# A graph-convolution kernel: groups gathered ahead from group 44 on, and tiles paired in one group of four

## The chip, the cores and the metric

The kernel runs on one core of a Trainium2 chip. Its engines work side by side, each through its own list of instructions in order: PE (TensorE, matmuls; its weight loads are listed apart as PEld), DVE (VectorE), ACT (ScalarE), POOL (GpSimd) and SP (SyncE, which issues loads and stores). The metric is the device time of one execution in microseconds; lower is better. The times before are the median of three runs.

## The reference

A layer of a graph network with 12500 nodes of 128 features and 400000 edges, sorted by `dst`:

```
h    = relu(layernorm(x))
W    = smu(edge_attr @ W_f1.T + b_f1) @ W_f2.T + b_f2      # smu: gelu-like, 20 -> 128 -> 128
W    = W * edge_weight[:, None]
msg  = (h @ W_in2f.T)[dst] * W                             # one message of 128 floats per edge
agg  = segment_sum(msg, src, 12500)                        # src is in no order
out  = x + smu(agg @ W_o1.T + b_o1) @ W_o2.T + b_o2
```

(In the code `src` and `dst` enter `_L0_gnn_ref` as `idx_i` and `idx_j`.) The gather goes by the sorted index, the sum by the random one.

## The kernel before

**Tiles, groups, epochs.** 128 edges make a tile, four tiles a group, two groups a super. There are 3125 tiles in 782 groups. The 98 blocks of 128 nodes are called bins. The sum over a random index is made in two passes: each message is first scattered to DRAM, into a buffer that is sorted by bin (`buf`), at a place counted out on the chip; later the buffer is read back bin by bin (`rw`), and a matmul with a one-hot matrix (`se`) adds up the rows of each node. `PARTS` cuts the edges into ten epochs, and while an epoch is scattered, the epoch before it is read back and summed (`add`, L1017). The supers of the last two epochs are spread among the others as "kept" groups: their messages wait in DRAM, and are scattered in a tail behind the last group.

**One group** takes these steps, each of which is a function of the group:

- `hide`, `bend`: the hidden layer (PE, L779, into the PSUM tile `pu`) and its gelu (ACT `ge`, L787);
- `pick_part`: the one-hot matrix `oh` for the gather (ACT, L578 and L579);
- `gather`, `take`: the rows of h by matmuls with `oh` (PE `ph`, L815) and their copy with the edge's weight (ACT `hg`, L834);
- `weigh`, `mix`: the filter (PE `pw`, L859 and L860) and the product (DVE `ms`, L889);
- `bins`, `count`, `read`, `number`: the place of each message within its bin (DVE `so`, L614; PE `pc`; DVE `sl`, L671; DVE `ix`);
- `send`, `scatter`: one indirect DMA a tile from POOL (L959) that writes 128 message rows to their places.

Messages have six buffers (`ms`), places (`ix`) eight.

**Pairs.** In one of `EVERY` groups, the messages of tiles 2 and 3 are moved into the rows of tiles 0 and 1 whose message goes into the same bin, so that one DMA writes two neighbouring rows. `spread_keys` (PE, L705) and `match` (DVE, L714, L719) find the partners, `rank_left` (PE, L726) and `place_left` (DVE, L733, L734) number those that have none, `permute` (PE, L746) moves the rows by matmuls into the PSUM tile `pt`, and `take_pairs` copies them out: `ms` (ACT, L759) for the second row of each pair, and `lt` (ACT, L760) for the left-over messages, with two small DVE instructions (`lat`, L756 and L757) for their bin and row. The left-overs are scattered with a later group, its `host`, and counted with it (L622). A paired group thus takes two double scatters, and its host one more.

**Order.** The kernel writes the order of every engine by hand: the loop over `p` calls the steps of different groups in a fixed order, and each engine takes its part of it in that order. Up to `p = AHEAD_FROM` the loop gathers and copies group p + 1, for which the product `mix(p + 1)` follows in the same turn. From there on it gathers p + 2, and hides and bends p + 3. Behind group 112, where `AHEAD_FROM` stands, the hidden layer takes turns in the PSUM banks `pu` and `pg1`, and the sums have `pg0` alone; before it, `pu` is alone and `pg0` and `pg1` take turns. `parts` puts off the start of a new bank of sums while `pu` has two banks. In the first epoch (up to group 112) there are no sums yet; there the loop does the preparation in small `step`s: layernorm and the rows of h, the reading of indices, the splitting of the edge features.

Of the kernel before, what the change touches and what calls it, by code (L numbers as in the profile page):

```python
# [15 lines left out]
ALU = mybir.AluOpType  # L16
# [14 lines left out]
GRP = 4  # L31
WIN = 42
PARTS = (56, 56, 56, 56, 46, 36, 36, 26, 16, 7)
EVERY = 5
WIDER = 0.17
SENT_LAST = 2
BUFS = 3
# [1 line left out]
ROW = P + 1  # L39
# [3 lines left out]
NOBIN = 200.0  # L43
NOBIN_ROW = float(1 << 17)
# [3 lines left out]
def gnn_kernel(  # L48
# [19 lines left out]
    nc = tc.nc  # L68
# [14 lines left out]
    PER = SUP // GRP  # L83
    NG = (NT + GRP - 1) // GRP
    eps_of, left = [], NS
# [9 lines left out]
    for a, n in eps_of:  # L95
        paired = n if len(CAP) < len(eps_of) - SENT_LAST else 0
# [100 lines left out]
    drow = const.tile([P, EPOCHS], F32, name="drow")  # L197
# [124 lines left out]
    with tc.tile_pool(name="ld", bufs=4) as ld, \  # L322
# [24 lines left out]
        pu_names = ["pu"]  # L347
# [151 lines left out]
        def at(p):  # L499
            return seq[p] if p < len(seq) else NG  # L500
# [10 lines left out]
        for p, g in enumerate(seq):  # L511
            if g // PER >= EARLY:
                continue
            since_pair += 1
            if wanting and p >= wanting[0][0] + 4:
                host[g] = wanting.pop(0)[1]
                assert epoch[g // PER] == epoch[host[g] // PER]
            elif since_pair >= EVERY and g > BY and g + 10 < ends_of[epoch[g // PER]]:
                paired[g] = len(paired)
                wanting.append((p, g))  # L520
                since_pair = 0
# [47 lines left out]
        def pick_part(g):  # L569

            if g >= NG:
                return
            s, i = divmod(g, PER)
            if i == 0:
                onehot[s] = edge.tile([P, SUP * P], BF, name="oh", bufs=3)
            o, n = i * GRP * P, groups[g][1] * P
            oh = onehot[s][:, o:o + n]
            nc.scalar.activation(oh, loaded[s][1][:, o:o + n], AF.Abs, bias=pneg if s < FEW // SUP else nrow)  # L578
            nc.scalar.activation(oh, oh, AF.Relu, scale=-1.0, bias=onesb[:, 0:1])  # L579
# [4 lines left out]
        def s_of(g):  # L584
            return g // PER
# [143 lines left out]
        def place_left(g):  # L729
# [5 lines left out]
                                    irow_ps.unsqueeze(1).to_broadcast([P, 2, P]),  # L735
                                    at_.unsqueeze(2).to_broadcast([P, 2, P]), op=ALU.is_equal)

        def permute(g):

            pp, cd = matched.pop(g)[1], apart_of.pop(g)  # L740
            po = ps1.tile([P, GRP * P], F32, name="pt")
            for j in range(3):
                w = ROW + 2 if j == 2 else ROW
                for i in range(2):
                    o = (4 + i if j == 2 else 2 * i + j) * P
                    nc.tensor.matmul(po[:, j * (ROW + 2):j * (ROW + 2) + w], pp[:, o:o + P], cd[:, i, :w],  # L746
                                     start=(i == 0), stop=(i == 1))
            matched[g] = po

        def take_pairs(g):  # L750

            po, ms, k = matched.pop(g), mixed[g], epoch[s_of(g)]
            lt = cnt.tile([P, ROW], F32, name="lt", bufs=2)
            at_ = cnt.tile([P, 2], F32, name="lat")
            o = 2 * (ROW + 2)
            nc.vector.tensor_scalar(at_[:, 0:1], po[:, o + ROW:o + ROW + 1], NOBIN, None, op0=ALU.add)  # L756
            nc.vector.tensor_scalar(at_[:, 1:2], po[:, o + ROW + 1:o + ROW + 2], NOBIN_ROW, drow[:, k:k + 1],  # L757
                                    op0=ALU.add, op1=ALU.min)
            nc.scalar.activation(ms[:, 1::2, :], po[:, :o].rearrange("p (j r) -> p j r", j=2)[:, :, 0:ROW], AF.Copy)  # L759
            nc.scalar.activation(lt, po[:, o:o + ROW], AF.Copy)  # L760
            left_of[g] = (lt, at_[:, 0:1], at_[:, 1:2])
# [28 lines left out]
        def smooth(g):  # L790
            if g >= NG:
                return
            if new(g):
                units_of.pop(g)
                return
            n = groups[g][1] * P
            sm = edge.tile([P, GRP * P], F32, name="sm", bufs=3)
            nc.vector.scalar_tensor_tensor(sm[:, :n], units_of.pop(g)[:, :n], LIN, hidden[g][:, :n],
                                           op0=ALU.mult, op1=ALU.add)
            hidden[g] = sm  # L800
# [25 lines left out]
        def take(g):  # L826
            if g >= NG:
                return
            n = groups[g][1] * P
            hg = edge.tile([P, GRP * P], F32, name="hg")  # L830
            if by_edge(g):
                t = groups[g][0]
                for j in range(groups[g][1]):
                    nc.scalar.activation(hg[:, j * P:(j + 1) * P], rows_of[g][:, j * P:(j + 1) * P], AF.Copy,  # L834
                                         scale=w_sb[:, t + j:t + j + 1])
                rows_of[g] = hg
                return
            nc.scalar.activation(hg[:, :n], rows_of[g][:, :n], AF.Copy)
            rows_of[g] = hg
# [77 lines left out]
        def send(g):  # L917

            if by_edge(g):
                scatter(g, mixed.pop(g))  # L920
                return
            t, n = groups[g]
            ms = msg.tile([P, GRP, ROW], F32, name="ms")
            places_in(g, ms)
            pt = mixed.pop(g)
            for j in range(n):
                nc.scalar.activation(ms[:, j, 0:P], pt[:, j], AF.Copy, scale=w_sb[:, t + j:t + j + 1])
            if s_of(g) >= EARLY:
                nc.scalar.dma_start(kept_rows[:, t - kept_tile:t - kept_tile + n, :], ms[:, :n, :])
                return  # L930
            scatter(g, ms)
# [543 lines left out]
            todo.setdefault(10 + i, []).append(f)  # L1475

        k = 0
        SOON, SLACK, AHEAD_FROM = 10, 40, eps_of[1][0] * PER
        for p in range(len(seq)):
            g = seq[p]  # L1480
            s = g // PER
            if p == (FEW // SUP - 3) * PER:
                assert not opening
            if p % PER == 0:
                load(sup_at(p // PER + 3))
            if s < EARLY:
                k = chores(g)
            else:
                lo = hi = done
            if SOON < p < SLACK:  # L1490
                turn(at(p))
                send(at(p))
            if p >= SLACK:
                if by_edge(g) and g not in paired:
                    send(g)
                if p > SLACK and not by_edge(at(p - 1)):
                    turn(at(p - 1))
                    send(at(p - 1))
            for f in todo.pop(p, []):
                f()  # L1500
            if p > AHEAD_FROM:
                smooth(at(p + 2))
            step()
            number(at(p + 1))
            weigh(at(p + 1))
            if at(p + 1) in paired:
                spread_keys(at(p + 1))
            if p <= AHEAD_FROM:
                gather(at(p + 1))
                take(at(p + 1))  # L1510
            parts(lo + (hi - lo) // 2)
            mix(at(p + 1))
            if g in paired:
                permute(g)
                take_pairs(g)
                send(g)
            if at(p + 1) in paired:
                match(at(p + 1))
            if p >= AHEAD_FROM:
                gather(at(p + 2))  # L1520
                take(at(p + 2))
            if p == 0:
                turn(at(1))
                send(at(1))
            if p >= SOON:
                step()
            if p <= AHEAD_FROM:
                hide(at(p + 2))
                bend(at(p + 2))
            else:  # L1530
                hide(at(p + 3))
                bend(at(p + 3))
            if p < SOON:
                step()
            count(at(p + 2))
            if p <= AHEAD_FROM:
                smooth(at(p + 2))
            if 0 < p < SOON:
                turn(at(p + 1))
                send(at(p + 1))  # L1540
                if p == 1:
                    pick_part(at(3))
            if p == AHEAD_FROM:
                assert taken_steps == COUNT
                pu_names[:] = ["pg1", "pu"]
                hide(at(p + 3))
                bend(at(p + 3))
            pick_part(at(p + 3 - (p == 0)))
            bins(at(p + 3))
            if at(p + 1) in paired:  # L1550
                rank_left(at(p + 1))
            read(at(p + 2))
            if at(p + 1) in paired:
                place_left(at(p + 1))
            parts(hi)
            step()
            assert k == 0 or taken_steps == COUNT
# [291 lines left out]
```

## Time and profile before

| | |
|---|---|
| runs | 4022.95, 4025.37, 4024.81 us; median 4024.81 |
| profiled execution | 4014.04 us, span 4012.3 us |
| busy share of the span | PE 83%, DVE 81%, POOL 74%, ACT 71% |
| mean granted clock of TensorE | 0.946 |
| scatters on POOL (L959) | 2694 + 181 of kept rows + 125 of left-overs |

The profile has a page for the whole execution and views that answer questions: groups of instructions by line, waits (who stood idle, for whom, how long in total, how many times, longest), busy time by windows, a timeline. "L959" is line 959 of the kernel before; `out<-in` names the tiles; x is a count. A scatter's time as counted on POOL does not hold the transfer itself.

### The profile page before, as it was taken

How to read it: one execution, taken by the hardware profiler on the slowest of the kernel's cores; microseconds unless marked ns; L12 is line 12 of the kernel's file. 1: busy time of each engine (PE TensorE's matmuls, PEld its weight loads, DVE VectorE, ACT ScalarE, POOL GpSimd, SP SyncE). 2: the span in 40 equal slices, each digit the busy share in tenths (PEclk: the TensorE clock that was granted, in tenths of full speed). 3: DMA queues.
4: the chain of work that ended last, by engine and by line, in shares of the span. 5: the costliest groups of instructions: out<-in, count | busy, mean ns of one | idle time of the engine just before them, and what ended most of it. 6: DMA issues, size and time to landing. Idle time of an engine off the chain costs nothing.

```text
span 4012.3 us, 85549 instructions
## 1 busy us (share of the span) xinstructions
PE 3315.2 (83%) x25912; PEld 2821.8 (70%) x26245; DVE 3264.7 (81%) x8658; ACT 2837.0 (71%) x7473; POOL 2949.5 (74%) x3044
## 2 busy tenths in 40 slices
PE   7766776888888888888888888888988888798658
PEld 4345655777777777777777777777887777687548
DVE  7886667888888888888888888888998888897447
ACT  6757787777877777788788887777777777675002
POOL 6765657777777777777777777777777777777776
PEclk9878788999999999999999999999999999999889
DMA  5775767888987777887787778877888777786878
GB/s 165 228 220 165 210 185 232 256 254 248 267 248 227 225 211 216 229 240 214 211 230 229 220 230 235 231 220 225 237 238 235 210 204 221 211 244 203 269 239 252
DMA packets 659903, 906.21 MB, mean 226 GB/s; under 512 B 181396, under 2 KB 446488, under 8 KB 659306
## 3 DMA queue, kind: packets, MB, share of 16 engines
q1 hardware_dynamic: 552009, 673.07, 59.1%
q0 software_dynamic: 100112, 215.31, 16.6%
q10 hardware_dynamic: 7312, 12.29, 0.9%
q8 instruction: 208, 3.41, 0.4%
q14 instruction: 262, 2.14, 0.2%
HBM read 507.13 MB, written 393.21 MB: 224 GB/s over the span
## 4 chain that ended last, share of the span: by engine, by line
PE 24%; DVE 16%; DMA 16%; ACT 11%; issue 9%; POOL 8%; SPq 1%; DVEq 0%; ACTq 0%; POOLq 0%
DMA buf<-ms,ix 12%; PE pg L1017 8%; POOL buf L959 8%; PE pw L859 6%; DVE so L614 4%; ACT hg L834 4%; DVE ms L889 3%; PE pt L746 2%; DVE se L1004 2%; ACT oh L578 2%; DVE sl L671 2%; ACT ge L787 2%; PE ph L815 2%; ACT oh L579 1%; DVE mt L714 1%
## 5 line engine op out<-in xcount | busy, mean ns | idle before, releaser
L959 POOL DMA_INDIRECT buf<-ms,ix x2694 | 2611.9, 970 | 944.3 <-issue 653.0
L1017 PE MATMUL pg<-se,rw 128*128 128x128 f32 x8232 | 1230.8, 290 | 118.1 <-DVE se L1004 66.2
L1017 PEld LDWEIGHTS pg<-se,rw 128*128 128x128 f32 x8232 | 1065.0, 198 | 190.2 <-issue 95.3
L859 PE MATMUL pw<-w_f,ge 128*128 128x128 f32 x5568 | 1025.8, 307 | 109.1 <-DVE ms L889 79.1
L834 ACT ACTIVATE hg<-ph,w_sb 128x128 f32<-128x128 f32 x2784 | 790.3, 368 | 331.4 <-PE ph L815 317.2
L859 PEld LDWEIGHTS pw<-w_f,ge 128*128 128x128 f32 x5568 | 880.6, 199 | 169.4 <-ACT ge L787 67.3
L614 DVE SCALAR_TENSOR_TENSOR so<-irow_ps,hi_f,so 128x98 f16<-128x98 f32 x2693 | 855.3, 318 | 73.9
L1004 DVE TENSOR_TENSOR se<-irow_ps,rw 128x1536 f32<-128x1536 f32 (+1 forms) x353 | 602.3, 1706 | 150.9 <-DMA rw<-buf 112.6
L860 PE MATMUL pw<-wls,f 128*128 128x128 bf16 x2784 | 625.4, 225 | 0.0
L579 ACT ACTIVATE oh<-oh,onesb 128x512 bf16<-128x512 bf16 x780 | 562.6, 721 | 25.4
L578 ACT ACTIVATE oh<-rbc,nrow 128x512 bf16<-128x512 uint8 x762 | 566.9, 744 | 2.4 <-DMA rbc<-rel_dram 2.4
L889 DVE TENSOR_TENSOR ms<-pw,hg 128x512 f32<-128x512 f32 x571 | 392.2, 687 | 202.2 <-ACT hg L834 81.4
L671 DVE TENSOR_REDUCE sl<-pc 128x4 f32<-128x392 f32 (+1 forms) x782 | 448.5, 573 | 11.8 <-PE pc L644 7.0
L815 PE MATMUL ph<-hw,oh 126*128 126x128 bf16 x2784 | 281.7, 225 | 105.7 <-ACT oh L579 100.3
L815 PEld LDWEIGHTS <-oh 126*128 126x128 bf16 x2784 | 198.7, 100 | 166.5 <-ACT oh L579 154.0
L787 ACT ACTIVATE ge<-pu 128x512 f32<-128x512 f32 x447 | 273.2, 611 | 22.0 <-PE pu L779 16.8
L860 PEld LDWEIGHTS <-f 128*128 128x128 bf16 x2784 | 286.9, 103 | 0.0
L759 ACT ACTIVATE ms<-pt 128x258 f32<-128x258 f32 x125 | 48.3, 386 | 312.5 <-DVE lat L757 283.8
L641 PE MATMUL pc<-so,tri 128*128 128x392 f16 (+1 forms) x611 | 211.5, 346 | 21.5 <-DVE sl L671 4.8
L959 POOL DMA_INDIRECT buf<-ms,ix_kept x181 | 176.0, 972 | 55.2 <-issue 53.7
L787 ACT ACTIVATE ge<-pg 128x512 f32<-128x512 f32 (+1 forms) x334 | 204.8, 613 | 0.0
L746 PE MATMUL pt<-cd,mt 128*128 128x129 f32 x1500 | 201.2, 286 | 0.9 <-DVE at L733 0.5
(315 smaller groups left out, 4292.3 us busy)
## 6 DMA issues: line engine op xcount, KB each, us to landing
rw<-buf SPq DMA_DIRECT2D x300, 774.0 KB
f<-f_parts SPq DMA_DIRECT2D x370, 240.0 KB
buf<-zero SPq DMA_DIRECT2D x146, 387.0 KB
rbc<-rel_dram SPq DMA_DIRECT2D x389, 128.0 KB
buf<-ms,ix POOLq DMA_INDIRECT x2694
f_parts<-hs SPq DMA_DIRECT2D x106, 360.0 KB
rw<-buf SPq DMA_DIRECT2D x49, 645.0 KB
f_parts<-hs SPq DMA_DIRECT2D x108, 240.0 KB
```

Source lines behind the costliest of these rows:

```text
L578: nc.scalar.activation(oh, loaded[s][1][:, o:o + n], AF.Abs, bias=pneg if s < FEW // SUP else nrow)
L579: nc.scalar.activation(oh, oh, AF.Relu, scale=-1.0, bias=onesb[:, 0:1])
L614: nc.vector.scalar_tensor_tensor(so[:, j], irow_ps[:, :NB], hi_f[:, t + j:t + j + 1], since, op0=ALU.is_equal, op1=ALU.add)
L671: nc.vector.tensor_reduce(sl[:, :n], pc[:, :n], op=ALU.max, axis=AX.X)
L787: nc.scalar.activation(ge[:, :n], units_of[g][:, :n], AF.Gelu, scale=ZS)
L815: nc.tensor.matmul(ph[:, j * P:(j + 1) * P], oh[:3 * WIN, a:a + P], hw[:3 * WIN, g % PER, :], start=True, stop=True)
L834: nc.scalar.activation(hg[:, j * P:(j + 1) * P], rows_of[g][:, j * P:(j + 1) * P], AF.Copy, scale=w_sb[:, t + j:t + j + 1])
L859: nc.tensor.matmul(pw[:, a:a + P], ge[:, a:a + P], w_f2, start=True, stop=False)
L860: nc.tensor.matmul(pw[:, a:a + P], fb[:, o + a:o + a + P], wls, start=False, stop=True)
L959: i = nc.gpsimd.indirect_dma_start(out=(wide if g in host or g in paired else bufs)[k][:, :], out_offset=bass.IndirectOffsetOnAxis(ap=ix, ...
L1004: nc.vector.tensor_tensor(se[:, a:a + n], own.unsqueeze(1).to_broadcast([P, n, P]), rows_in[c][:, a:a + n, P:P + 1].to_broadcast([P, n, P] ...
L1017: nc.tensor.matmul(pgs[0][:, g, :], rows_in[c][:, o, 0:P], sel[c][:, o, :], start=(q == 0), stop=(q == Q[k] - 1))
```

## The change

Four edits go together:

1. `AHEAD_FROM` is 44 instead of 112: gathering two groups ahead and hiding three ahead begins at group 44. The hidden layer keeps the one bank `pu`, and the sums take turns in `pg0` and `pg1`, to the end.
2. `EVERY` is 4 instead of 5, and a host follows its pair by three groups instead of four. 155 groups are paired instead of 125. The sizes of the buffers come out the same.
3. In the loop, `permute`, `take_pairs` and `send` of a paired group come behind `match` of the next and behind `gather` and `take` of p + 2.
4. The two `lat` instructions are taken out of `take_pairs` into `number_left`, which is called just ahead of `bins(p + 3)`.

```diff
-EVERY = 5
+EVERY = 4
...
-            if wanting and p >= wanting[0][0] + 4:
+            if wanting and p >= wanting[0][0] + 3:
...
+        left_at = {}
+
+        def number_left(g):
+
+            (po, at_), k = left_at.pop(g), epoch[s_of(g)]
+            nc.vector.tensor_scalar(at_[:, 0:1], po[:, 0:1], NOBIN, None, op0=ALU.add)
+            nc.vector.tensor_scalar(at_[:, 1:2], po[:, 1:2], NOBIN_ROW, drow[:, k:k + 1], op0=ALU.add, op1=ALU.min)
...
             o = 2 * (ROW + 2)
-            nc.vector.tensor_scalar(at_[:, 0:1], po[:, o + ROW:o + ROW + 1], NOBIN, None, op0=ALU.add)
-            nc.vector.tensor_scalar(at_[:, 1:2], po[:, o + ROW + 1:o + ROW + 2], NOBIN_ROW, drow[:, k:k + 1],
-                                    op0=ALU.add, op1=ALU.min)
+            left_at[g] = (po[:, o + ROW:o + ROW + 2], at_)
...
-        SOON, SLACK, AHEAD_FROM = 10, 40, eps_of[1][0] * PER
+        SOON, SLACK, AHEAD_FROM = 10, 40, 44
...
-            if p > AHEAD_FROM:
-                smooth(at(p + 2))
             step()
             number(at(p + 1))
...
             mix(at(p + 1))
-            if g in paired:
-                permute(g)
-                take_pairs(g)
-                send(g)
             if at(p + 1) in paired:
                 match(at(p + 1))
             if p >= AHEAD_FROM:
                 gather(at(p + 2))
                 take(at(p + 2))
+            if g in paired:
+                permute(g)
+                take_pairs(g)
+                send(g)
...
             if p == AHEAD_FROM:
-                assert taken_steps == COUNT
-                pu_names[:] = ["pg1", "pu"]
                 hide(at(p + 3))
                 bend(at(p + 3))
             pick_part(at(p + 3 - (p == 0)))
+            if g in paired:
+                number_left(g)
             bins(at(p + 3))
```

(`smooth` emits nothing for the groups from 40 on.)

## The prediction

> **What bounds the kernel now.** I read the page first, then cut the span into stages, then asked for the waits of each stage.
>
> ```profile
> span 4012.3 us, 85549 instructions
> ...
> L959 POOL DMA_INDIRECT buf<-ms,ix x2694 | 2611.9, 970 | 944.3 <-issue 653.0
> ...
> L815 PE MATMUL ph<-hw,oh 126*128 126x128 bf16 x2784 | 281.7, 225 | 105.7 <-ACT oh L579 100.3
> ...
> L759 ACT ACTIVATE ms<-pt 128x258 f32<-128x258 f32 x125 | 48.3, 386 | 312.5 <-DVE lat L757 283.8
> ...
> L746 PE MATMUL pt<-cd,mt 128*128 128x129 f32 x1500 | 201.2, 286 | 0.9 <-DVE at L733 0.5
> ```
>
> No engine looks full, but POOL's line says why: one scatter (L959) is counted busy 970 ns, and the idle time before it is mostly "issue", that is, POOL waits for nothing the profile shows. So the pace of scatters has to be taken from start to start. The view of busy time by windows does it. I cut at the times when the 50th and 100th, the 112th and the 586th group of the order are read out (L671); for each engine it gives the busy time and, as x, the number of instructions; POOL stands last before the granted clock, and nearly all of its instructions are scatters.
>
> ```profile
> core 0: us, PE busy (x) PEld busy (x) DVE busy (x) ACT busy (x) POOL busy (x), PEclk, DMA share, GB/s
> 283.00:596.00 313.00, 227.59 (x1419) 183.06 (x1435) 196.73 (x614) 242.60 (x634) 182.49 (x189) 0.79 0.62 186
> 649.00:2757.00 2108.00, 1820.32 (x14992) 1579.07 (x15203) 1823.05 (x4932) 1647.64 (x4410) 1586.05 (x1634) 0.98 0.80 233
> 2757.00:3700.00 943.00, 813.85 (x6876) 728.90 (x6969) 805.80 (x2097) 677.11 (x1784) 716.40 (x742) 0.97 0.76 222
> 3100.00:3600.00 500.00, 420.52 (x3521) 372.96 (x3570) 421.19 (x1116) 360.89 (x949) 379.94 (x394) 0.97 0.75 217
> 3710.00:3940.00 230.00, 148.19 (x966) 130.16 (x967) 107.19 (x110) 14.60 (x25) 175.05 (x180) 0.83 0.84 260
> 661.00:680.00 19.00, 14.20 (x122) 11.56 (x124) 15.87 (x52) 17.44 (x50) 14.43 (x16) 1.00 0.74 222
> ```
>
> In 3100:3600 a scatter comes every 500/394 = 1.269 us. In the tail, 3710:3940, with DVE and ACT nearly out of it, it is 230/180 = 1.278. So about 1.27 us is POOL's own pace, whoever else works. By that measure: 2757:3700 takes 943/742 = 1.271, POOL is the bound. 649:2757 takes 2108/1634 = 1.290, 2108 − 1634 × 1.269 = 34 us above the pace: nearly bound by POOL, but DVE and PE are also at 86% each. 283:596 takes 313/189 = 1.656: 313 − 189 × 1.269 = 73 us above the pace. There POOL is starved, and the waits say by what:
>
> ```profile
> POOL buf L959 <- issue: 82.1, 142, 8.5
> DVE ms L889 <- ACT hg L834: 55.2, 23, 6.4
> ACT hg L834 <- PE ph L815: 52.7, 31, 6.0
> PEld pw L859 <- ACT ge L787: 36.4, 26, 2.8
> DVE cd L877 <- ACT hg L834: 29.1, 10, 5.7
> ```
>
> In 283:596 the same group's gather, its copy with weights (hg) and its product follow each other with nothing between: ACT waits 53 us for PE, and DVE then 55 + 29 = 84 us for ACT. From group 112 on the gather is done one group ahead.
>
> **Part 1, the early stage.** The change starts the order "one group ahead" at group 44. What DVE waits for hg (84 us of 313) goes. Next late is either POOL or ACT. POOL: the changed program has 155 paired groups where it was 125, and by place in the order 13, 99 and 43 of them lie before 112, in 112 to 586 and after, where it was 10, 80 and 35. Each saves one scatter (two double ones and one for the left-overs replace four). So (189 − 3) × 1.269 = 236 us by POOL. ACT is busy 242.6 us here, with the preparation of the h rows in it. A paired group costs ACT two copies and some small ones more; at most four at L759's 0.386 us, 1.5 us, three times 1.5: 247 us. An ACT that is the bound needn't be full: the densest stretch that I found after group 112, 661:680, has 17.44/19 = 92%. 247/0.92 = 268 us. Thus −45 us, with bounds of −77 (313 − 236, POOL's pace) and −15 (half of the freed DVE wait is taken by the next wait of the chain and ACT stays at 82%: an estimate, from the 36 us that PE's weight loads wait for ge and the 53 us that ACT waits for ph). In 253:283 and 596:649 nothing is to be had that I would count.
>
> **Part 2, more pairs, in 112 to 586.** POOL loses 19 scatters: 19 × 1.269 = 24 us. The other engines gain work.
>
> ```profile
> L889 DVE TENSOR_TENSOR ms<-pw,hg 128x512 f32<-128x512 f32 x571 | 392.2, 687 | 202.2 <-ACT hg L834 81.4 <-DMA buf<-ms,ix 45.6 <-issue 17.8
> ...
> L714 DVE SCALAR_TENSOR_TENSOR mt<-pt,key,onesb 128x256 f32<-128x256 f32 x250 | 110.1, 478 | 10.6 <-PE pt L705 10.3
> ...
> L734 DVE TENSOR_TENSOR mt<-irow_ps,at 128x256 f32<-128x256 f32 x125 | 53.1, 425 | 4.3
> L877 DVE TENSOR_TENSOR cd<-pw,hg 128x256 f32<-128x256 f32 x125 | 52.2, 418 | 38.7 <-ACT hg L834 35.2 <-PE pw L860 3.1
> L878 DVE TENSOR_TENSOR ms<-pw,hg 128x256 f32<-128x256 f32 x125 | 52.0, 416 | 11.8 <-DMA buf<-ms,ix 11.5 <-issue 0.2
> L622 DVE SCALAR_TENSOR_TENSOR so<-irow_ps,lat,so 128x98 f16<-128x98 f32 x125 | 40.0, 320 | 4.4
> ```
>
> DVE for one more pair: 2 × 0.478 + 0.425 + 0.418 + 0.416 − 0.687 (the one product that it replaces) + 0.320 = 1.85 us, and some eight small instructions (at, lat twice, the accumulators, the doubled counts) of which none is above L622's 0.320; at half of that 1.3 us, so 3.2 us, and 19 × 3.2 = 61 us. PE: 201.2/125 = 1.61 us for L746, and less than a third of that again for the spreading of keys and the longer counts (an estimate), so 2.1 us and 40 us in all.
>
> **Part 3, the order around a pair.** Two things move. ACT's copies after a pair (L759) no longer wait for DVE's two small "lat" instructions, which move to a place of their own; and the gather of the group after next, with ACT's copy of it, now comes ahead of the permuting matmuls.
>
> ```profile
> ACT ms L759 <- DVE lat L757: 191.0, 72, 6.1
> ...
> PE ph L815 <- ACT oh L579: 82.5, 117, 2.1
> ...
> DVE lat L756 <- PE pt L746: 51.3, 49, 2.2
> PE pt L726 <- DVE h_first L719: 42.4, 31, 2.5
> DVE agg L1030 <- PE pg L1017: 27.3, 34, 5.1
> ```
>
> These are waits of 649:2757. ACT loses 191 us at L759, 2.65 us a time; what stands behind it in ACT's queue is hg, ge and the one-hot oh, and PE then waits 82.5 us for oh. With ACT free earlier I expect most of these 82.5 us to go. Against it: in DVE's queue "lat" still stands straight behind the product and ahead of the next group's counts (L614), and its matmuls now end one gather later, 281.7/696 = 0.40 us (four matmuls to a group). Where DVE waits there already, it waits 0.40 us longer: at most 99 × 0.40 = 40 us, and about half of it, 20 us, as 49 of the 80 pairs wait now and PE will run earlier. The left-overs are now taken in three groups behind their pair instead of four; their count (L622) stands behind "lat" on the same engine and waits for nothing new. POOL's scatters and SP's loads keep their order.
>
> **Part 4, the PSUM banks.** After group 112 the hidden layer had two banks and the sums one; now it is the other way round. A sum no longer stops for DVE's addition, and the rule that put off the start of a bank because of it no longer applies. The single bank of the hidden layer costs nothing: PE reaches the next hide only behind a gather that needs oh, and ACT makes that oh after it has read the bank (ge). If the gather did not stand ahead, PE would stop there in each group for something like the 36.4/26 = 1.4 us that its weights wait for ge in 283:596.
>
> **Sum for 112 to 586.** PE's account: +40 − 82 = −42 us. DVE's: +61 + 20, less what DVE itself waits for PE (51 + 27 us) as far as an earlier PE shortens it, so between +3 and +81. POOL can take −59 at most (2108 − 1615 × 1.269). DVE's account decides, and I take its lower end, 0, because the waits it holds are for just the engine that is relieved. Bounds −59 and +81.
>
> **Part 5, after 586.** POOL is the bound; 8 scatters less, 8 × 1.27 = −10 us. The cover is that the others run ahead until they find no free message buffer:
>
> ```profile
> ACT ms L937 <- DMA buf<-ms,ix: 49.3, 30, 5.3
> ACT ms L881 <- DMA buf<-ms,ix: 32.9, 19, 4.4
> ```
>
> ACT alone stands 82 us in 2757:3700 at buffers whose scatters haven't landed. DVE's extra, 8 × 3.2 + 43 × 0.40 = 43 us, fits into that. Without this cover it would be +33 instead of −10. The tail behind the last group (3700 on) has no pairs and stays.
>
> **Sum:** −45 + 0 − 10 = −55 us. The profiled execution took 4014.0 us with a span of 4012.3 us, so it would take 3959; the median of the runs is 4024.8, 10.8 above the profiled one, so 3970 us as a median.
>
> **The rivals.**
>
> *DVE becomes the bound (slower).* Speaking for it: DVE and PE are at 86% in 649:2757, and the change gives DVE 61 us there and puts its wait for the permute behind a gather. If the relief of PE doesn't reach DVE: +81 us in the middle; after 586 the cover fails, up to +33; the early stage gives back its lower end, −15 to −45. With −45 that is +69, 4094 us as a median; with half of the middle, 4050. It decides as soon as DVE's net in the middle is above the 55 us of the other stages. Against it: the stretch after 2757 holds the pace of 1.27 with DVE at 85% too. Chance 0.16.
>
> *POOL paces all.* Every stage falls to 1.27 us a scatter: −77 − 59 − 10 = −146, 3879 us. For it: 649:2757 is only 34 us above the pace now. Against it: ACT at 242.6 us in the early stage against POOL's 236. Chance 0.12.
>
> *The early stage keeps its time.* The clock granted to PE is 0.79 there, and the preparation interrupts every engine; only −15 us come, and the middle loses 15. In sum −10 us, 4015: at the edge of what a measurement can tell. Chance 0.12.
>
> *DVE's work slows the scatters themselves.* By the traces the pace is 1.269 with DVE at 84% and 1.278 with DVE at 47% (107.19/230), so DVE doesn't slow POOL, and I give it 0.02. If it did, the 30 × 3.2 = 96 us that DVE gains would stand in POOL's way and, with −38 for the scatters and −45 early, the time would be about 4038 us. [...]
>
> **How the numbers follow.** The forecast has 0.58. About 0.2%, 8 us, is what a measurement of this kernel can tell from no change. Faster: the forecast, POOL's pace, and somewhat under half of the third case, 0.75. Same: the other part of it, 0.07. Slower: 0.18. The forecast alone reaches from 3930 (−20 more in the early stage, −20 in the middle) to 4010 (+40 in the middle). To leave out no more than 2 in 10 the range goes down to 3900, into POOL's pace, and up to 4040, through the milder half of DVE as the bound.
>
> **What would show it.** Right: 186 scatters in the stretch of groups 50 to 100 take about 268 us instead of 313, with ACT above 90% and hardly a wait of DVE for hg; "ACT ms <- DVE lat" is gone, and PE's wait for oh is under 30 us in the middle; DVE's wait at lat is above 51 us; after group 586 the pace is 1.27 again and waits for message buffers remain. Wrong: if the pace in the middle is above 1.32 us a scatter (1615 × 1.32 = 2132, +24 us), DVE's account decided; if the early stage takes over 295 us, ACT wasn't what came next.

## The result, and the profile after

The changed kernel takes 4042.9 us (median of 6 runs, 4041.1 to 4045.3), the kernel before 4025.9 (6 runs beside them, 4023.0 to 4030.6): ratio 1.0041, 95% interval 1.0029 to 1.0053. It is slower by 17 us; the forecast was 55 us faster, with a chance of 0.18 for slower.

The profiled execution has a span of 4041.4 us. The page, with lines that answer to those shown of before (L959 is now L965, L759 is L765, L746 is L754):

```profile
span 4041.4 us, 87287 instructions
...
L965 POOL DMA_INDIRECT buf<-ms,ix x2634 | 2553.4, 969 | 982.4 <-issue 614.8
...
L821 PE MATMUL ph<-hw,oh 126*128 126x128 bf16 x2784 | 283.8, 226 | 79.3 <-ACT oh L579 72.5
```

60 scatters fewer in this row (with 30 left-over ones more that have a row of their own), 58 us less of POOL's time, and yet more idle time before them. Where it arose shows in the windows, cut at the same groups as before (50, 100, 112, 586 and the last):

```profile
core 0: us, PE busy (x) PEld busy (x) DVE busy (x) ACT busy (x) POOL busy (x), PEclk, DMA share, GB/s
280.00:553.00 273.00, 208.38 (x1477) 165.35 (x1477) 202.20 (x653) 243.49 (x644) 182.12 (x186) 0.86 0.72 209
553.00:620.00 67.00, 37.88 (x256) 29.01 (x255) 37.61 (x115) 41.28 (x108) 45.38 (x47) 0.77 0.69 200
620.00:2792.00 2172.00, 1881.86 (x15479) 1633.32 (x15479) 1861.49 (x5182) 1678.44 (x4496) 1557.18 (x1609) 0.97 0.80 226
2792.00:3726.00 934.00, 825.63 (x7119) 742.15 (x7119) 826.57 (x2225) 690.34 (x1828) 709.55 (x737) 0.98 0.80 226
```

The prediction cut the kernel before at 2757; the read-out of group 586 is at 2751, so that its middle was 6 us shorter, and the last stage as much longer, than it said. Cut there, before:

```profile
649.00:2751.00 2102.00, 1816.36 (x14968) 1575.96 (x15179) 1817.20 (x4916) 1645.21 (x4401) 1581.36 (x1630) 0.98 0.80 233
2751.00:3700.00 949.00, 817.81 (x6900) 732.01 (x6994) 811.64 (x2113) 679.54 (x1793) 721.09 (x747) 0.97 0.76 222
```

Groups 50 to 100: 273 us instead of 313. Groups 100 to 112: 67 instead of 53. The middle, 112 to 586: 2172 instead of 2102, at 2172/1609 = 1.350 us a scatter instead of 2102/1630 = 1.290. After 586: 934 instead of 949, at 1.267 a scatter, POOL's own pace. In sum −40 + 14 + 70 − 15 = +29, which is the difference of the two spans; what lies before group 50 and behind the last cancels. (The profiled execution before was 11 us under its median, that of the changed kernel at its median; so 17 us of medians stand beside 29 us of spans.) The middle lost what the early stage won, and more. Its waits:

```profile
POOL buf L965 <- issue: 393.1, 1107, 9.4
ACT hg L840 <- PE ph L821: 332.6, 295, 10.6
DVE lat L743 <- ACT lt L766: 122.1, 77, 5.6
PE pw L865 <- DVE ms L895: 91.1, 83, 8.3
...
PE ph L821 <- ACT oh L579: 38.0, 47, 3.3
POOL buf L965 <- ACT ms L945: 36.3, 28, 7.9
```

The third line is new. Before, ACT waited at its copies for lat, 191 us; now DVE waits at lat for ACT's copies, 122 us, where it waited 51 us for PE. As expected, PE's wait for oh fell (82.5 to 38.0, though not under the 30 that the prediction named). In its place PE waits for DVE's product: 91 us, and 19.0 before (`PE pw L859 <- DVE ms L889` in the same window). And POOL now waits for messages. The same place in time, first before, then after (start, duration, engine, line):

```profile
2217.24 0.69 DVE L889 TENSOR_TENSOR ms<-pw,hg 128x512 f32<-128x512 f32 x1
...
2217.71 1.51 PE L746 MATMUL pt<-cd,mt 128*128 128x129 f32 x12
...
2219.05 0.39 PE L815 MATMUL ph<-hw,oh 126*128 126x128 bf16 x4
...
2219.25 0.16 DVE L756 TENSOR_SCALAR lat<-pt 128x1 f32<-128x1 f32 x1 [1.32 <-PE pt L746]
...
2219.63 0.39 ACT L759 ACTIVATE ms<-pt 128x258 f32<-128x258 f32 x1 [1.66 <-PE ph L815]
```

```profile
2219.04 0.39 PE L821 MATMUL ph<-hw,oh 126*128 126x128 bf16 x4
...
2219.26 1.56 PE L754 MATMUL pt<-cd,mt 128*128 128x129 f32 x12
2219.46 1.14 ACT L840 ACTIVATE hg<-ph,w_sb 128x128 f32<-128x128 f32 x4 [1.49 <-PE ph L821]
...
2220.86 0.39 ACT L765 ACTIVATE ms<-pt 128x258 f32<-128x258 f32 x1 [0.25 <-PE pt L754]
...
2221.14 0.27 ACT L766 ACTIVATE lt<-pt 128x129 f32<-128x129 f32 x1
...
2221.45 0.16 DVE L743 TENSOR_SCALAR lat<-pt 128x1 f32<-128x1 f32 x1 [0.43 <-ACT lt L766]
...
2221.65 0.31 DVE L614 SCALAR_TENSOR_TENSOR so<-irow_ps,hi_f,so 128x98 f16<-128x98 f32 x1
```

Before, lat starts 0.03 us after the permute's end (2217.71 + 1.51 = 2219.22). After, the permute ends at 2220.82, and lat starts 0.63 us later, behind both copies. Both read the same PSUM tile, `pt`, each its own columns. In this program the later reader in the written order waits for the earlier one, though neither uses the other's result: ACT for lat before (283.8 us in the whole execution), DVE for ACT's copies now (183.4). The runs only move this wait; none shows what would come of it if the order were dropped. The next group's counts (L614) stand behind it on DVE.

### The profile page after: what moved, and what is told of

Its sections match the earlier page's. It is cut to its first block, busy times and chain, and to the rows that moved or that the text cites. A ratio compares the mean times of both kernels' runs of the same rounds, so it can differ in the third digit from the quotient of the medians.

```text
span 4041.4 us, 87287 instructions
## 1 busy us (share of the span) xinstructions
PE 3371.5 (83%) x26725; PEld 2873.5 (71%) x26725; DVE 3329.9 (82%) x9078; ACT 2884.4 (71%) x7623; POOL 2920.1 (72%) x3014
## 5 line engine op out<-in xcount | busy, mean ns | idle before, releaser
L965 POOL DMA_INDIRECT buf<-ms,ix x2634 | 2553.4, 969 | 982.4 <-issue 614.8
L614 DVE SCALAR_TENSOR_TENSOR so<-irow_ps,hi_f,so 128x98 f16<-128x98 f32 x2633 | 836.6, 318 | 73.0
L793 ACT ACTIVATE ge<-pu 128x512 f32<-128x512 f32 x781 | 476.0, 609 | 30.2 <-PE pu L785 29.5
L895 DVE TENSOR_TENSOR ms<-pw,hg 128x512 f32<-128x512 f32 x541 | 371.3, 686 | 99.8 <-issue 18.3
L821 PE MATMUL ph<-hw,oh 126*128 126x128 bf16 x2784 | 283.8, 226 | 79.3 <-ACT oh L579 72.5
L785 PE MATMUL pu<-f,w1s 128*128 128x512 bf16 x742 | 293.8, 396 | 11.5 <-DMA f<-f_parts 10.9
L821 PEld LDWEIGHTS <-oh 126*128 126x128 bf16 x2784 | 211.7, 101 | 125.3 <-ACT oh L579 106.8
L754 PE MATMUL pt<-cd,mt 128*128 128x129 f32 x1860 | 243.3, 280 | 1.4 <-ACT ms L933 1.4
L754 PEld LDWEIGHTS pt<-cd,mt 128*128 128x128 f32 x1860 | 223.0, 193 | 3.4 <-ACT ms L933 1.8
L965 POOL DMA_INDIRECT buf<-ms,ix_kept x181 | 176.4, 974 | 55.2 <-issue 54.3
```

The costliest lines, as they stand in the source:

```text
L614: nc.vector.scalar_tensor_tensor(so[:, j], irow_ps[:, :NB], hi_f[:, t + j:t + j + 1], since, op0=ALU.is_equal, op1=ALU.add)
L821: nc.tensor.matmul(ph[:, j * P:(j + 1) * P], oh[:3 * WIN, a:a + P], hw[:3 * WIN, g % PER, :], start=True, stop=True)
L965: i = nc.gpsimd.indirect_dma_start(out=(wide if g in host or g in paired else bufs)[k][:, :], out_offset=bass.IndirectOffsetOnAxis(ap=ix, ...
```

## The experiments

Two theories. A: lat behind ACT's copies is what the middle pays for. B: the 30 further pairs are, by their own work on DVE and PE, whatever the order. Ratios are to the kernel before, run on the same chip beside them, with 95% intervals. Four of these kernels also ran on two other chips, which the last part of this section tells of; what is compared ran on chips where the kernel before takes about 4020 us (medians of 4017 to 4030).

**One pair in five, the rest changed** (`EVERY = 5`, host four groups behind).

```diff
-EVERY = 4
+EVERY = 5
...
-            if wanting and p >= wanting[0][0] + 3:
+            if wanting and p >= wanting[0][0] + 4:
```

> The change with one pair in five and the host four groups behind, as before; all else stays changed. Theory A (DVE's small lat instructions now stand behind ACT's copies, 183 us of waits in the changed kernel): the wait stays at each of 125 pairs, about 1.2 us each, so the middle (groups 112 to 586) is still slower than before by 20 us or more, the early stage keeps its 25 us, and the time is 4020 to 4035. Theory B (the 30 further pairs' own work on DVE is the price, whatever the order): the middle falls back to 2102 us or below, and the time is 3990 to 4000.

3990.4 us, ratio 0.9931 (0.9918 to 0.9944). B's number. But the middle isn't "2102 or below": it takes 2110, and DVE still waits 156 us for ACT's copies (`ACT lt L766: 156.1, 102`):

```profile
617.00:2727.00 2110.00, 1827.78 (x15167) 1582.42 (x15167) 1814.65 (x4914) 1656.37 (x4400) 1579.49 (x1630) 0.98 0.80 232
```

With 125 pairs and this wait the kernel is faster than before; with 155 it is slower. So the number of pairs matters, but this doesn't tell whether as work or as waits. The edit also puts the host back to four groups behind its pair; no run here moves the host alone.

**One pair in four alone**, in the kernel before (the same two lines, the other way round).

> The kernel before with one pair in four and the host three groups behind, nothing else. Theory A: the pairs alone cost little, since ACT waits for lat and not DVE for ACT; POOL's 38 us and DVE's 96 us nearly cancel: 4015 to 4035. Theory B: the middle takes 60 us more, 10 us come back after group 586: 4065 to 4080.

4037.2 us, ratio 1.0049 (1.0035 to 1.0063), between the two and close to A's upper end. The middle takes 2123 us (+21), and the stage after 586 takes 945 (−4) where POOL's pace promised −10. Here DVE waits at lat for PE alone, 72.7 us.

```profile
651.00:2774.00 2123.00, 1847.88 (x15473) 1598.06 (x15471) 1859.06 (x5180) 1661.66 (x4495) 1562.57 (x1611) 0.98 0.79 231
```

More pairs don't pay in the old order, but they cost far less in the middle than the 70 us of the change.

**Lat ahead of the copies**, the rest changed.

```diff
             left_at[g] = (po[:, o + ROW:o + ROW + 2], at_)
+            number_left(g)
...
-            if g in paired:
-                number_left(g)
             bins(at(p + 3))
```

> The changed kernel with the two lat instructions written ahead of ACT's copies again, as before, so that ACT waits for DVE and not DVE for ACT; pairs still permuted behind the gather. Theory A: DVE's wait at lat falls from 183 us to what the permute itself makes it wait, 100 us or less, and the time falls by 40 to 70 us, to 3975 to 4005. Theory B: within 8 us of the changed kernel's 4043.

3996.4 us, ratio 0.9944 (0.9930 to 0.9958): A's range. The view of the tile lat, what DVE waited for there and who waited for lat:

```profile
its engine sat idle before it (us, times) until:
  PE pt L754: 106.1, 92
  issue: 0.9, 1
who waited for it (us, times):
  ACT ms L766: 121.1, 139
```

The wait has turned round again, with the order of the two lines: ACT waits for lat, DVE only for PE. The middle takes 2118 us instead of 2172.

**Lat where it is used**, the rest changed.

```diff
             if g in host:
+                number_left(host[g])
                 last[k] = so[:, GRP]
...
-            if g in paired:
-                number_left(g)
             bins(at(p + 3))
```

> The changed kernel with the lat instructions written directly ahead of the count that needs them (L622), behind the four counts of the host's own tiles (1.28 us). Neither engine should then wait long for the other. Theory A: DVE's wait at lat falls below 60 us, and the time to 3960 to 3995, below that with the lat first. Theory B: within 8 us of 4043.

3969.4 us, ratio 0.9875 (0.9858 to 0.9893): A's range. The four counts of the host's own tiles now cover most of the wait:

```profile
its engine sat idle before it (us, times) until:
  ACT lt L767: 44.5, 59
  ACT ms L766: 1.3, 2
```

```profile
284.00:557.00 273.00, 213.84 (x1468) 170.62 (x1468) 200.54 (x649) 242.51 (x643) 180.21 (x185) 0.83 0.70 208
621.00:2718.00 2097.00, 1855.78 (x15474) 1615.40 (x15473) 1850.49 (x5180) 1678.23 (x4496) 1562.12 (x1609) 0.98 0.80 234
2718.00:3650.00 932.00, 825.18 (x7122) 744.26 (x7121) 823.30 (x2226) 689.13 (x1828) 707.65 (x732) 0.98 0.78 226
```

The middle takes 2097 us with the pairs, the scatters and the work of the changed kernel (DVE 1850 us busy, there 1861). 75 us hang on where two instructions of 0.16 and 0.21 us stand.

**Lat where it is used, one pair in five** (both edits).

> The changed kernel with lat at its use and one pair in five. It prices the 30 further pairs where DVE hardly waits for ACT's copies. If POOL's 38 us are then worth having, it is slower than the ratio 0.9875 of one in four: 0.990 to 0.996. If DVE's 96 us still outweigh them, it is faster: 0.975 to 0.985.

3976.7 us, ratio 0.9888 (0.9864 to 0.9912): not told apart from 0.9875, so neither half of the expectation came. The middle is the same too:

```profile
617.00:2714.00 2097.00, 1828.69 (x14958) 1597.19 (x15169) 1809.54 (x4916) 1658.54 (x4400) 1577.57 (x1627) 0.97 0.80 233
```

Where DVE hardly waits at lat, the 30 further pairs are worth nothing that could be measured here, one way or the other. (With the host four groups behind, lat at its use stands a whole turn of the loop later than with three, and DVE doesn't wait for ACT's copies at all.)

The changed kernel and three of the variants so far, all with the gather ahead of the permute, make a table of ratio and middle:

| | lat behind ACT's copies | lat where it is used |
|---|---|---|
| one pair in five | 0.9931, 2110 us | 0.9888, 2097 us |
| one pair in four | 1.0041, 2172 us | 0.9875, 2097 us |

The wait costs 0.4% with 125 pairs and 1.7% with 155. The further pairs cost 1.1% with the wait and nothing that shows without it. The two together cost more than their sum.

**The early start alone**, in the kernel before.

```diff
-        SOON, SLACK, AHEAD_FROM = 10, 40, eps_of[1][0] * PER
+        SOON, SLACK, AHEAD_FROM = 10, 40, 44
...
             if p == AHEAD_FROM:
-                assert taken_steps == COUNT
-                pu_names[:] = ["pg1", "pu"]
                 hide(at(p + 3))
                 bend(at(p + 3))
+            if p == eps_of[1][0] * PER:
+                pu_names[:] = ["pg1", "pu"]
```

> The kernel before with the early start at group 44 alone; the banks change over at group 112 as before. The early stage (groups 50 to 100) should fall from 313 to 275 us, with 5 to 15 us lost again in groups 100 to 112, and the middle stay at 2101: ratio 0.990 to 0.995. If part of that gain came from the order around the pairs, it is less than half: ratio above 0.996.

3995.1 us, ratio 0.9937 (0.9919 to 0.9955), in the range expected. Groups 50 to 100 take 284 us (not 275), 100 to 112 57 (4 more than before, where 5 to 15 were expected), the middle 2110, 8 above the kernel before.

**The banks alone**, in the kernel before (the line `pu_names[:] = ["pg1", "pu"]` left out).

> The kernel before with the banks of the change alone: one bank for the hidden layer, two for the sums, throughout. PE's 48 us of waits for the addition of sums should fall below 12, and the time by 0 to 20 us (ratio 0.995 to 1.000), if the single bank costs nothing. If it costs, ratio above 1.002, and PE waits at hide for ge.

4036.3 us, ratio 1.0013 (1.0001 to 1.0025): nothing gained, perhaps 5 us lost, in neither of the two ranges. PE's wait for the sums' addition nearly went (`PE pg L1017 <- DVE agg L1030`, 46.2 to 7.7 us in the whole execution), but it waits longer for DVE's product (`PE pw L859 <- DVE ms L889: 101.5`, 79.1 before). The hide waited for ge once, 1.4 us.

**Pairs ahead of the gather again**: edits 3 and 4 undone, banks, early start and one in four kept.

```diff
             mix(at(p + 1))
+            if g in paired:
+                permute(g)
+                take_pairs(g)
+                send(g)
             if at(p + 1) in paired:
                 match(at(p + 1))
...
-            if g in paired:
-                permute(g)
-                take_pairs(g)
-                send(g)
```

(with the two edits of lat ahead of the copies.)

> The changed kernel with edits 3 and 4 undone: permute, lat and ACT's copies stand ahead of match and of the gather again, as before; early start, banks and one pair in four stay. If the gather ahead of the permute costs DVE its 0.40 us at each of 155 pairs: faster than the 0.9944 of lat first, ratio 0.982 to 0.990. If the gather ahead is worth more to ACT and PE: ratio 0.996 to 1.002.

4022.4 us, ratio 0.9978 (0.9968 to 0.9988), against 0.9944 with the gather ahead: the gather ahead gains 0.3%, some 14 us. DVE waits longer at lat with it (106 us against 78), as the prediction had it, but PE waits 81 us for oh at the gather (L822) instead of 152. Without edits 3 and 4 the middle takes 2135 us:

```profile
632.00:2767.00 2135.00, 1842.07 (x15259) 1604.30 (x15470) 1863.03 (x5180) 1663.95 (x4496) 1553.74 (x1606) 0.98 0.81 229
```

The changed kernel stands at 1.0041, so edits 3 and 4 together cost 0.6%: the gather ahead gains 0.3%, and lat behind ACT's copies loses 1%.

**The same with lat where it is used.**

> The changed kernel with lat at its use (ratio 0.9875) and edit 3 undone: pairs permuted and copied ahead of match and the gather. DVE no longer waits at lat, so DVE's 0.40 us are no issue; what is left is ACT's and PE's side. If the gather ahead helps ACT, this is slower: 0.990 to 0.997. If the order doesn't matter once DVE is free: 0.985 to 0.990.

3990.8 us, ratio 0.9894 (0.9877 to 0.9910), against 0.9875: the intervals overlap, the order of gather and permute isn't told apart there.

**The keys spread later**: lat where it is used, and the spreading of the keys behind the first half of the sums.

```diff
-            if at(p + 1) in paired:
-                spread_keys(at(p + 1))
...
             parts(lo + (hi - lo) // 2)
+            if at(p + 1) in paired:
+                spread_keys(at(p + 1))
```

> The changed kernel with lat at its use, and the spreading of the keys (L705) behind the first half of the sums instead of ahead of it. PE waits 96 us for the keys in that kernel. If that wait is on the path, most of 60 us in the middle goes: ratio 0.970 to 0.982. If the match behind it then only waits for PE instead, as DVE has little else to do there, the ratio stays at 0.985 to 0.990.

3979.4 us, ratio 0.9870 (0.9855 to 0.9885). PE's wait for the keys fell from 96 to 43 us, and the time stayed. So taking that wait out of the way gained nothing.

**Four kernels on two other chips.** There the kernel before took 5948.5 and 5944.5 us, and stood in waits that the profile puts down to nothing in the program. In the view of waits of the early start alone on such a chip:

```profile
ACT hg L834 <- remote: 1142.3, 207, 11.6
DVE sl L671 <- remote: 408.4, 82, 9.3
```

First chip, pairs ahead of the gather, the early start alone, the banks alone, and lat at its use with one pair in five:

> The changed kernel with edits 3 and 4 undone: permute, the two lat instructions and ACT's copies stand ahead of match and of the gather again, as before; early start, banks and one pair in four stay. Compared with the kernel that only has lat ahead of ACT's copies (ratio 0.994 to before): if the gather ahead of the permute costs DVE its 0.40 us at each of 155 pairs, this one is faster by 20 to 50 us, ratio 0.982 to 0.990. If the gather ahead is worth more to ACT and PE (PE waited 116 us for oh in the kernel with the pairs alone, 88 us with lat first) than it costs DVE, it is slower, ratio 0.996 to 1.002.

> The kernel before with the early start at group 44 alone; the banks change over at group 112 as before. The early stage (groups 50 to 100) should fall from 313 to 275 us, with 5 to 15 us lost again in groups 100 to 112, and the middle stay at 2101: ratio 0.990 to 0.995. If part of that gain came from the order around the pairs, it is less than half: ratio above 0.996.

> The kernel before with the banks of the change alone: one bank for the hidden layer, two for the sums, throughout. PE's 48 us of waits for the addition of sums should fall below 12, and the time by 0 to 20 us (ratio 0.995 to 1.000), if the single bank of the hidden layer costs nothing, as the prediction argued. If it costs, ratio above 1.002, and PE waits at hide for ge.

> The changed kernel with lat at its use and one pair in five. It prices the 30 further pairs where DVE no longer waits for ACT's copies. With lat at its use and one in four the ratio to before was 0.9875. If POOL's 38 us are then worth having, this one is slower than that: ratio 0.990 to 0.996. If DVE's 96 us still outweigh them, it is faster: ratio 0.975 to 0.985.

The ratios were 0.9882 (0.9856 to 0.9908), 0.9952 (0.9932 to 0.9971), 0.9995 (0.9979 to 1.0011) and 1.0081 (1.0053 to 1.0109). Second chip, two of them once more:

> Once more the changed kernel with lat at its use and one pair in five, on a chip that runs the kernel before in some 4020 us. It prices the 30 further pairs where DVE hardly waits for ACT's copies. If POOL's 38 us are then worth having, it is slower than the ratio 0.9875 of one in four: 0.990 to 0.996. If DVE's 96 us still outweigh them, it is faster: 0.975 to 0.985.

> Once more the changed kernel with edits 3 and 4 undone (pairs permuted and copied ahead of the gather, lat ahead of the copies), on such a chip. If the gather ahead of the permute costs DVE its 0.40 us at each pair: faster than the 0.9944 of lat first, ratio 0.982 to 0.990. If the gather ahead is worth more to ACT and PE: ratio 0.996 to 1.002.

1.0078 (1.0050 to 1.0105) and 0.9866 (0.9836 to 0.9897). The two chips agree with each other, but not with the others on these two kernels (0.9888 and 0.9978). Where the kernel takes nearly half as long again and stands in waits from elsewhere, the balance that this document is about can't be read; nothing here is explained from these runs, and what makes these chips wait stays open.

## Why the prediction was wrong

- **POOL's pace, and that the early stage starves on hg: right.** (Only DVE is not "nearly out of" the tail that it compares: it is busy 47% there.) −45 was forecast for groups 50 to 100, −40 came, with ACT at 243.49/273 = 89% as what came next (above 90% was expected). DVE's long waits for hg are gone there. The early start alone gives 0.6%.
- **"In 253:283 and 596:649 nothing is to be had that I would count": wrong by 14 us.** Groups 100 to 112 take 67 us instead of 53. Among their waits are two for DMA. In the same groups before, the first came to 0.2 us and the second did not occur:

```profile
PE pu L785 <- DMA f<-f_parts: 10.9, 4, 6.0
...
ACT hs L264 <- DMA h_dram<-hs: 9.5, 2, 6.9
```

The edge features (`f`) and the last of the h rows (`hs`) come and go by DMA, and a stage that reaches them earlier would wait for them. That fits, but isn't shown to be the cause: PE waits about as long for oh (12.4 us), and its granted clock in these groups is 0.77, before 0.90. The other kernels that have the early start lose there too: 4 to 8 us with one pair in five, 10 to 15 with one in four. Why the pairs matter there stays open.
- **Part 3, the order around a pair: the step that failed.** It held that lat's only loss was the gather of 0.40 us ahead of the permute, and put lat's wait for ACT's copies at nothing. ACT's wait for lat did go, but it was a matter of order between two readers of one PSUM tile, and it turned round with the order: DVE waits 122 us in the middle, all of it for ACT, not 51 + 20 for PE. The profile had shown the sign of it: ACT waited 284 us for lat without using it. Lat ahead of the copies again gives 0.9944, and lat where it is used 0.9875, with everything else of the change in place. So the prediction's sign "DVE's wait at lat is above 51 us" came by luck: it was meant for the gather, and what came was the wait for ACT. Its sign of being wrong, a pace above 1.32 us in the middle, came with 1.350.
- **The sum for the middle: 0 forecast, +70 measured.** DVE's account was the one that decided, as the text said, but its lower end (+3 by its own terms, taken as 0) was chosen on the ground that an earlier PE would shorten DVE's waits. PE did get earlier at oh, and DVE's waits for PE were replaced by one for ACT. DVE's work was sized too high: it is busy 1861 − 1817 = 44 us more (61 forecast). PE is busy 1882 − 1816 = 66 us more (40 forecast), but only 32 and 39 more in two kernels with as many pairs and faster middles (1848 with one pair in four alone, 1856 with lat at its use), so the work itself was sized about right. With lat at its use, the stages come out near the forecast: −40 in groups 50 to 100, −5 in the middle and −17 after 586, where −45, 0 and −10 were forecast, and +10 in groups 100 to 112, which it had left out.
- **The size of the rival.** "DVE becomes the bound" named the stage (+81 at the most, +70 came) with a chance of 0.16, and put its price down to work. The runs show work and the wait together: the wait with 125 pairs leaves the middle at 2110, and 155 pairs with little or nothing of it leave it at 2097 to 2135, depending on the order. Against POOL's pace (scatters × 1.269), the middle stands 34 us above it before, 42 with one pair in five, 55 with lat at its use, 79 with one pair in four alone, and 130 in the changed kernel. Why the two costs don't simply add up stays open. One might think of the lead over POOL, which shows as waits of ACT and DVE for a free message buffer: while there is a lead, a wait on DVE would cost nothing. Over the whole execution these waits do fall, from 156 us before to 58 in the changed kernel (145 with one pair in five, 146 with lat at its use, 93 with one pair in four alone). But in the middle, where the loss is, they hardly differ: 26 us before, 32 with one pair in five, 21 with lat at its use, 19 in the changed kernel. So they don't show the cause. The distance of the host, three groups or four, goes with the number of pairs in these kernels and wasn't tested by itself.
- **Part 4, the banks: right that the single bank costs hardly a wait (1.4 us); freeing PE from the addition, to which it gave no price, gained nothing.** PE's wait for DVE's product grew instead, by 22 us.
- **Part 5: right.** −10 was forecast, −15 came, and ACT still waits 24 us for message buffers there (82 before).
- **DVE's work slowing the scatters: no.** The pace after 586 is 934/737 = 1.267 with DVE at 89% (826.57/934), before 949/747 = 1.270 with DVE at 86% (811.64/949).

The version that beats both kernels is the change with lat where it is used: 0.9875, some 50 us under the kernel before.

## What to carry to other kernels

Before an instruction is moved, look at what it shares with its neighbours on other engines, not only at what it needs: in this kernel a wait between two readers of one PSUM tile went to whichever came second in the program (ACT, 284 us before; DVE, 183 us in the changed kernel), and moving it from an engine with room (ACT, 71% busy) to one that decides the pace (DVE, 81%) was a loss (ratio 1.0041, and 0.9944 with lat ahead of the copies). A wait that the profile shows for an engine whose result isn't used, as ACT's for lat, is the warning. And costs of two changes needn't add up: here the wait cost 0.4% with 125 pairs and 1.7% with 155, so each is best measured with the other in place and without it.

## What was not expected of the hardware

POOL's scatters came 1.267 to 1.278 us apart, from start to start, in the stretches measured here in which they were fed, with DVE busy 47% to 89% of the time. That some write two neighbouring rows to a place and not one doesn't show in it: the stage after 586 has 43 pairs instead of 35 and the same pace, 1.267 and 949/747 = 1.270, and the tail without pairs 1.278.
